# Dealing edges into buckets: running counts moved to TensorE, buffers and table pieces redistributed, loads of the joint stage reordered

## The chip, the core and the metric

The kernel runs on one core of a Trainium2 chip. Its engines are called here as the profile calls them: PE is TensorE's matmul (PEld its weight loads), DVE is VectorE, ACT is ScalarE, POOL is GpSimd, SP is SyncE, and a "q" behind a name marks a DMA issue on that engine's queue. The metric is the device time of one execution in microseconds (us), as a median of several. All times within a profile count from the start of the span of one profiled execution.

## The reference

A graph with N = 3125 nodes of 256 features and E = 53125 directed edges (with self loops) goes through four layers. The change touches the first of them and what feeds it:

```python
h        = relu(concat(node[src], node[dst], edge_attr) @ mW1 + mb1)   # per edge, 512 units
messages = h @ mW2 + mb2
agg      = segment_sum(messages, src, num_segments=N)
u        = relu(concat(node, agg) @ uW1 + ub1) @ uW2 + ub2
x        = x + node + u                                                # node = layernorm(x)
```

Three more layers follow: a mixture of four experts, two graph convolutions over the same edges (segment sums over the edge list, done as products with a dense matrix of edge counts), and a feed-forward layer for half of the tokens. None of these is changed.

## The kernel before

The first product is split: `concat(node[src], node[dst], edge_attr) @ mW1` is a table row of the source (`tab_a`), plus a table row of the target (`tab_b`), plus a small product of the edge's 16 attributes. Each table has one row of 512 values for each node. `tab_h` holds `tab_a` in two halves (a rounded value and the rest), and `w_h` holds the 16 rows of weights of the attributes in two halves as well.

**Dealing, `deal()`.** Edges are sorted by source into 98 buckets of 32 nodes. The edge list is laid out as 416 tiles of 128 edges, taken in 104 chunks of four. For each chunk:

- `buckets(c)` compares bucket numbers with a row of ids on DVE (`oh`, one-hot, 128 x 4 x 98, L340) and adds up, in four DVE adds (`so_far`, L346 and L350), how many edges of each bucket each partition had in all tiles before.
- `select(c)` makes two products on PE (L363, L364): a triangular matrix `later` with `oh`, and a matrix of ones with `so_far`. Their sum in PSUM is, for each edge and bucket, the number of edges before it.
- `place(c)` picks each edge's own bucket (`own`, L371; `ranks`, L374), computes its place in the buffer (L376 to L382, `to`) and builds the row to be stored: `rt`, of which DVE makes the one-hot source part (L385) and ACT copies attributes and target (L107). `to` and `rt` are rings of six buffers each.
- `put(c)` stores the four tiles with four indirect DMAs of POOL (L394) to `cbuf`, in HBM; each takes 128 rows to 128 computed places.

In the first 13 chunks `halve_attributes` also turns the edges' attributes on PE and splits them in two halves (L298 on ACT, L299 on DVE).

**Tables, `tables()`.** A generator in four pieces for each of 25 blocks of 128 nodes: layernorm rows on DVE (with one square root on ACT); turning them on PE and copying (ACT); the products with `mW1` on PE (L313), followed for `tab_a` by the addition of the bias on DVE (L316, the bias `mb1` loaded as 128 copies of its row), the rounded half on ACT (L318) and the rest on DVE (L319), and for `tab_b` by a copy on ACT; and five DMA writes on SP (L325 to L329). From chunk 4 on, two pieces are taken after each chunk, so a block takes two chunks and the tables end half way through the dealing.

The order of instructions on PE, DVE, ACT and SP is the order of the program text there: the loop calls `buckets(c+2)`, `select(c+1)`, `put(c)`, `place(c+1)`, then the table pieces. Behind the last chunk come the counts of all buckets and checks on DVE (`count` to `fits`, L422 to L447), and the writing of `w_h` (L450 to L454). `fits` decides at a branch which of two joint stages runs; here it is the fast one.

**Joint stage, `edges_by_bucket()`.** A unit g is a group of four buckets; it is worked on in five steps (ROUNDS). `begin(g)` loads with SP the unit's rows of `tab_h` (`gives`, two DMAs of 256 KB, L698) and its edges (`rows`, 680 KB, L700). `goes` (DVE, L706) makes indices from them, `fetch` gathers `tab_b` rows by four indirect DMAs of 256 KB a step on POOL (L713), three steps ahead, into four buffers. `turned` turns the one-hot and attribute part on PE (L735) and copies it on ACT (`oT`, L107), `spread` multiplies it by `gives` (PE, L752), `hidden_units` adds the gathered rows (DVE, L758), ACT applies the relu (L763) and `by_source` sums by source (PE, L769). From the second unit on, `counts` (the dense matrix of edge counts) and the nodes' own work run in between. `goes(1)` stands in the text behind the hidden units of step 2 and ahead of those of step 3; `begin(1)` stands in step 0.

Ahead of the steps, `rest_of(fast)` issues on ACT's queue 26 loads of weights and biases for the nodes' work (L468 to L497), then four zero fills of the count matrix (L680 to L686, also ACT); SP issues `begin(0)` and eight copies of `w_h` into `gives` (L842).

Of the kernel before, what the change touches and what calls it, by code (L numbers as in the profile page):

```python
# [8 lines left out]
F32 = mybir.dt.float32  # L9
# [7 lines left out]
P = 128  # L17
# [33 lines left out]
def gnn_ffn_kernel(ctx: ExitStack, tc: tile.TileContext, a: dict, out: bass.AP):  # L51
# [125 lines left out]
    def deal():  # L177
# [46 lines left out]
        for k in range(0, NB - 1, 8):  # L224
            nc.sync.dma_start(x[:, k:k + 8, :], a["x"][k * P:(k + 8) * P].rearrange("(k p) d -> p k d", p=P))
            if k == 0:
                mw1 = tp.tile([P, 4, HID], F32, name="mw1", bufs=1)
                nc.sync.dma_start(mw1, a["L0_gnn_mW1"][0:2 * D].rearrange("(k p) m -> p k m", p=P))
                mb1 = tp.tile([P, HID], F32, name="mb1", bufs=1)
                b = a["L0_gnn_mb1"]  # L230
                nc.sync.dma_start(mb1, bass.AP(tensor=b.tensor, offset=b.offset, ap=[[0, P], [1, HID]]))
                w_ea = tp.tile([32, HID], F32, name="w_ea", bufs=1)
                for i in range(2):
                    nc.sync.dma_start(w_ea[16 * i:16 * (i + 1)], a["L0_gnn_mW1"][2 * D:2 * D + 16])
# [67 lines left out]
        def tables():  # L302
            for k in range(NB):
                xns = layernorm_rows(k, 1, True, nc.vector)
                yield
                xT = tp.tile([P, 2, P], F32, name="xTa")
                layernorm_turn(xns, xT)
                yield
                ts = []
                for h in range(2):  # L310
                    pp = bank("pp")
                    for c in range(2):
                        nc.tensor.matmul(pp, lhsT=xT[:, c, :], rhs=mw1[:, 2 * h + c, :], start=c == 0, stop=c == 1)  # L313
# [12 lines left out]
                nc.sync.dma_start(tab_a[rows, :], ts[0])  # L326
                nc.sync.dma_start(tab_h[rows, 0, :], first.bitcast(F32))
                nc.sync.dma_start(tab_h[rows, 1, :], rest.bitcast(F32))
                nc.sync.dma_start(xT0[:, :, rows], xT)  # L329
                yield  # L330


        with tc.tile_pool(name="deal", bufs=3) as dp:
            chunks = ET // GB
            ohs, pos, rts = {}, {}, {}

            def buckets(c):

                oh = dp.tile([P, GB, NBK], F16, name="oh", bufs=4)
                nc.vector.tensor_tensor(oh, ids[:, :NBK].unsqueeze(1).to_broadcast([P, GB, NBK]),  # L340
                                        bk[:, c * GB:(c + 1) * GB].unsqueeze(2).to_broadcast([P, GB, NBK]), op=OP.is_equal)
                so_far = dp.tile([P, GB, NBK], F16, name="so_far", bufs=4)
                with nc.allow_low_precision("whole numbers up to 416"):
                    if c:
                        oh_, last = ohs[c - 1]
                        nc.vector.tensor_tensor(so_far[:, 0], last[:, GB - 1], oh_[:, GB - 1], op=OP.add)  # L346
                    else:
                        nc.vector.memset(so_far[:, 0], 0.0)
                    for i in range(1, GB):
                        nc.vector.tensor_tensor(so_far[:, i], so_far[:, i - 1], oh[:, i - 1], op=OP.add)  # L350
                ohs[c] = oh, so_far

            def edges_before(some):
                pk = bank("pk")
                nc.tensor.matmul(pk[:, :NBK], lhsT=ones, rhs=some, start=True, stop=True)
                return pk[:, :NBK]

            def select(c):

                oh, so_far = ohs[c]  # L360
                pk = bank("pk")
                out = pk[:, :GB * NBK].rearrange("p (g b) -> p g b", g=GB)
                nc.tensor.matmul(out, lhsT=later, rhs=oh, start=True, stop=False)  # L363
                nc.tensor.matmul(out, lhsT=ones, rhs=so_far, start=False, stop=True)  # L364
                return out

            def place(c, out):
                oh = ohs[c][0]
                at = slice(c * GB, (c + 1) * GB)
# [34 lines left out]
            for c in range(-1, chunks):  # L404
# [17 lines left out]
            oh, so_far = ohs[chunks - 1]  # L422
            run = dp.tile([P, NBK], F16, name="run", bufs=1)
            with nc.allow_low_precision("whole numbers up to 416"):
                nc.vector.tensor_tensor(run, so_far[:, GB - 1], oh[:, GB - 1], op=OP.add)
            count = dp.tile([P, NBK], F32, name="count", bufs=1)
            nc.vector.tensor_copy(count, edges_before(run))
            most = dp.tile([P, NBK], F32, name="most", bufs=1)
            nc.vector.tensor_scalar(most, count, float(CAP), None, op0=OP.is_gt, op1=OP.add, accum_out=bad[:, 0:1])
            nc.vector.tensor_scalar(most[:, :full * GB], count[:, :full * GB], float(SURE * P), None, op0=OP.is_lt, op1=OP.add,  # L430
                                    accum_out=bad[:, 1:2])

# [15 lines left out]


            wf, wr = [dp.tile([32, HID], F32R, name=f"w_{j}", bufs=1) for j in "hl"]  # L450
            nc.scalar.activation(wf, w_ea, AF.Copy)
            nc.vector.tensor_tensor(wr, w_ea, wf.bitcast(F32), op=OP.subtract)
            nc.sync.dma_start(w_h[:, 0, :], wf.bitcast(F32))
            nc.sync.dma_start(w_h[:, 1, :], wr.bitcast(F32))  # L454
        prep.close()
# [5 lines left out]
    def rest_of(fast):  # L461
# [211 lines left out]
        def edges_by_bucket():  # L673
            with tc.tile_pool(name="bk", bufs=2) as bp, tc.tile_pool(name="upd", bufs=2) as up, \
# [4 lines left out]

                for hf, w in ((half0, W0), (half1, W1)):  # L680
                    left = NP - NBK * BN
                    flat = hf[NBK * BN:, :].rearrange("s (h l) -> (s h) l", l=w)
                    cn = bp.tile([P, W1], F16, name="cn", bufs=5)
                    nc.vector.memset(cn, 0.0)
                    for o in range(0, 4 * left, P):
                        nc.scalar.dma_start(flat[o:o + P, :], cn[:, :w])  # L686

                gives = [bp.tile([P, 2, 2, HID], F32R, name=f"gives{i}", bufs=1) for i in range(2)]  # L690

                def begin(g):
                    nb = min(4, NBK - 4 * g)
                    ag = gives[g % 2]
                    for i in range(2):
                        src = bass.AP(tensor=tab_h.tensor, offset=tab_h.offset + (g * P + i * BN) * 2 * HID,
                                      ap=[[2 * HID, BN], [4 * BN * HID, nb // 2], [1, 2 * HID]])
                        nc.sync.dma_start(ag[2 * BN * i:2 * BN * i + BN, :nb // 2].bitcast(F32).rearrange("p i c h -> p i (c h)"), src)  # L698
                    rows = bp.tile([P, PER, RW], F32R, name="rows", bufs=3)
                    nc.sync.dma_start(rows.bitcast(F32).rearrange("p r w -> p (r w)"),  # L700
                                      cbuf[g * P * PER:(g + 1) * P * PER, :].rearrange("(p r) w -> p (r w)", p=P))
                    return dict(g=g, nb=nb, m=nb * BN, ag=ag, rows=rows, oa={}, ob={})
# [136 lines left out]
                for t in gives:  # L839
                    for at in (BN, 3 * BN):  # L840
                        for i in range(2):
                            nc.sync.dma_start(t[at:at + 32, i].bitcast(F32), w_h[:])  # L842


# [537 lines left out]
```

## Time and profile before

| | |
|---|---|
| runs | 2400.23, 2407.05 and 2401.82 us; median 2401.82 |
| the profiled execution | 2503.9 us, its span 2501.8 us |
| mean granted PE clock | 0.832 |
| busy in the span | PE 1836.7 us (73%), DVE 1549.4 (62%), POOL 987.6 (39%), ACT 876.3 (35%) |

The stages, with the share of time in which each engine was busy in them:

| stretch, us | what runs | PE | DVE | ACT | POOL | DMA | clock |
|---|---|---|---|---|---|---|---|
| 0 to 32 | loads, `cbuf` cleared, first chunks placed | 0.24 | 0.89 | 0.15 | 0.09 | 0.88 | 1.00 |
| 32 to 84 | dealing, attributes halved, first tables | 0.35 | 0.55 | 0.17 | 0.61 | 0.59 | 0.80 |
| 692 to 1790 | joint stage: edges, counts, nodes | 0.89 | 0.63 | 0.52 | 0.47 | 0.56 | 0.87 |
| 1790 to 1917 | last nodes, hand-over to the convolutions | 0.76 | 0.40 | 0.37 | 0.12 | 0.23 | 0.87 |
| 1917 to 2274 | two convolutions | 0.98 | 0.67 | 0.37 | 0.07 | 0.50 | 0.97 |
| 2274 to 2502 | ranking and the last layer | 0.80 | 0.54 | 0.18 | 0.00 | 0.04 | 0.90 |

The rest of the dealing and the hand-over (84 to 692) are taken up in the prediction. A row of the profile's table of groups reads: line, engine, operation, tile written and tiles read, count, then total busy time and the mean in nanoseconds of one, then the idle time of the engine just before such instructions and what ended it. Three groups of the dealing, over 0 to 660 us, are:

| group | count | busy us | mean ns |
|---|---|---|---|
| L350 DVE add, `so_far` | 312 | 66.4 | 213 |
| L346 DVE add, `so_far` of the next chunk | 103 | 21.1 | 205 |
| L313 PE, products of the tables | 200 | 133.1 | 826 |

A timeline row gives the start, the duration (of several merged instructions together, with their count behind an x), and in brackets how long the engine had been idle and what ended that. The name of a releaser is inferred from semaphore events; "issue" means that nothing in the profile ended the wait.

### The profile page before, as it was taken

How to read it: one execution, taken by the hardware profiler on the slowest of the kernel's cores; microseconds unless marked ns; L12 is line 12 of the kernel's file. 1: busy time of each engine (PE TensorE's matmuls, PEld its weight loads, DVE VectorE, ACT ScalarE, POOL GpSimd, SP SyncE). 2: the span in 40 equal slices, each digit the busy share in tenths (PEclk: the TensorE clock that was granted, in tenths of full speed). 3: DMA queues.
4: the chain of work that ended last, by engine and by line, in shares of the span. 5: the costliest groups of instructions: out<-in, count | busy, mean ns of one | idle time of the engine just before them, and what ended most of it. 6: DMA issues, size and time to landing. Idle time of an engine off the chain costs nothing. (4 is left out here: it accounts for less than half of the span.)

```text
span 2501.8 us, 26233 instructions
## 1 busy us (share of the span) xinstructions
PE 1836.7 (73%) x7873; PEld 1091.7 (44%) x7873; DVE 1549.4 (62%) x4427; ACT 876.3 (35%) x1553; POOL 987.6 (39%) x1032
## 2 busy tenths in 40 slices
PE   3455551111078898898898998898885999999689
PEld 1222220000034454455454454454454777886356
DVE  7687775555255665665665665665644676667931
ACT  1211110000045555555555555554433333343111
POOL 4566666766545444445444444444300000110000
PEclk9687775555568889889889899899897999999889
DMA  8233330000666556555555555555304444650000
GB/s 265 96 129 124 119 118 25 25 24 26 167 201 196 146 159 173 161 162 178 157 158 165 150 178 165 149 172 169 114 26 125 120 129 119 169 145 1 0 34 19
DMA packets 231403, 309.98 MB, mean 124 GB/s; under 512 B 34392, under 2 KB 165315, under 8 KB 230884
## 3 DMA queue, kind: packets, MB, share of 16 engines
q1 hardware_dynamic: 167296, 153.00, 20.8%
q0 software_dynamic: 52512, 142.96, 19.6%
q10 hardware_dynamic: 11444, 12.27, 1.6%
q8 instruction: 64, 1.05, 0.2%
q14 instruction: 87, 0.71, 0.1%
HBM read 226.44 MB, written 81.69 MB: 123 GB/s over the span
## 5 line engine op out<-in xcount | busy, mean ns | idle before, releaser
L713 POOL DMA_INDIRECT cb<-tab_b,goes_to x490 | 477.4, 974 | 617.8 <-issue 275.1
L394 POOL DMA_INDIRECT cbuf<-rt,to x416 | 416.3, 1001 | 233.3 <-issue 197.1
L758 DVE TENSOR_TENSOR cb<-pa,cb 128x1024 f32<-128x1024 f32 x245 | 288.7, 1218 | 263.2 <-PE pa L752 190.1
L1277 PE MATMUL padj<-z,slab 128*128 128x512 f32 x1250 | 321.4, 410 | 16.0 <-DVE z L1186 16.0
L763 ACT ACTIVATE cb<-cb 128x1024 f32<-128x1024 f32 x245 | 257.6, 1051 | 94.7 <-DVE cb L758 72.9
L1277 PEld LDWEIGHTS padj<-z,slab 128*128 128x128 f32 x1250 | 233.2, 192 | 75.4 <-issue 24.1
L752 PE MATMUL pa<-gives,oT 64*128 64x512 f32 x980 | 188.7, 506 | 36.1 <-ACT oT L107 34.3
L133 PE MATMUL pt<-ident,xn 128*128 128x128 f32 x200 | 49.5, 339 | 218.8 <-DVE xn L122 130.3
L363 PE MATMUL pk<-oh,later 128*128 128x392 f16 x104 | 47.2, 454 | 190.3 <-DVE oh L340 95.0
L810 PE MATMUL pn<-ob,oa 128*128 128x448 f16 (+1 forms) x692 | 165.6, 363 | 20.6 <-ACT cn L107 7.5
L125 POOL TENSOR_TENSOR x<-x,xn 128x256 f32<-128x256 f32 x25 | 24.4, 978 | 352.7 <-DVE xn L122 352.7
L795 DVE TENSOR_SCALAR ob<-ids,rows 128x448 f16<-128x448 f16 (+1 forms) x490 | 163.3, 333 | 0.0
L791 DVE TENSOR_SCALAR oa<-ids,rows 128x128 f16<-128x128 f16 x692 | 163.0, 262 | 0.0
L752 PEld LDWEIGHTS pa<-gives,oT 64*128 64x128 f32 x980 | 105.8, 231 | 101.2 <-ACT oT L107 43.8
L769 PE MATMUL ph<-cb,rows 128*32 128x512 f32 x980 | 144.8, 645 | 0.0
L107 ACT ACTIVATE oT<-pt 64x256 fp32r<-64x256 f32 (+1 forms) x250 | 93.1, 373 | 134.9 <-DMA cb<-tab_b,goes_to 72.2
L107 ACT ACTIVATE cn<-pn 128x352 f16<-128x352 f32 x196 | 98.3, 502 | 118.0 <-PE pn L810 91.0
L313 PE MATMUL pp<-mw,xTa 128*128 128x512 f32 x200 | 133.1, 826 | 0.2 <-issue 0.2
L133 PEld LDWEIGHTS pt<-ident,xn 128*128 128x128 f32 x200 | 24.8, 160 | 243.1 <-DVE xn L122 129.5
L107 ACT ACTIVATE rt<-row 128x144 f32<-128x144 f32 x104 | 32.8, 319 | 258.7 <-DMA cbuf<-rt,to 208.1
L506 PE MATMUL pd<-xT,fw 128*128 128x512 f32 (+1 forms) x224 | 91.8, 566 | 35.4 <-DVE y L1328 35.4
L735 PEld LDWEIGHTS pt<-ident_r,rows 128*128 128x128 f32 x490 | 67.1, 198 | 110.4 <-issue 69.4
(221 smaller groups left out, 3137.4 us busy)
## 6 DMA issues: line engine op xcount, KB each, us to landing
two<-adj_h SPq DMA_DIRECT2D x24, 1600.0 KB
rows<-cbuf SPq DMA_DIRECT2D x25, 680.0 KB
gives<-tab_h SPq DMA_DIRECT2D x48, 256.0 KB
adj_h<-cn SPq DMA_DIRECT2D x98, 112.0 KB
adj_h<-cn SPq DMA_DIRECT2D x98, 88.0 KB
cb<-tab_b,goes_to POOLq DMA_INDIRECT x490
cbuf<-rt,to POOLq DMA_INDIRECT x416
cbuf<-empty ACTq DMA_DIRECT2D x4, 1632.0 KB
```

The lines of the kernel that those rows point to most:

```text
L107: nc.scalar.activation(dst, src, AF.Copy)
L313: nc.tensor.matmul(pp, lhsT=xT[:, c, :], rhs=mw1[:, 2 * h + c, :], start=c == 0, stop=c == 1)
L394: one_of = nc.gpsimd.indirect_dma_start(out=cbuf[:], out_offset=bass.IndirectOffsetOnAxis(ap=to[:n, i:i + 1], axis=0), in_=rt[:n, i, :], i ...
L713: nc.gpsimd.indirect_dma_start(out=cb[:, j, :], out_offset=None, in_=tab_b[:], in_offset=bass.IndirectOffsetOnAxis(ap=u["to"][:, i:i + 1], ...
L752: nc.tensor.matmul(got[j // 2][:, j % 2, :], lhsT=oT[at, j // 2, :], rhs=u["ag"][at, j // 2, c, :], start=c == 0, stop=c == 1)
L758: nc.vector.tensor_tensor(cb[:, j:j + 2], pa, cb[:, j:j + 2], op=OP.add)
L763: nc.scalar.activation(h, h, AF.Relu)
L769: nc.tensor.matmul(u["ph"][j * BN:(j + 1) * BN, :], lhsT=u["rows"][:, GB * r + j, :BN].bitcast(F32), rhs=hs[j // 2][:, j % 2, :], start=r ...
L791: nc.vector.tensor_scalar(oa, ids[:, 1 + i * P:1 + (i + 1) * P], field[:, 0:1], None, op0=OP.is_equal)
L795: nc.vector.tensor_scalar(ob[:, :w], ids[:, 1:w + 1], field[:, 1:2], None, op0=OP.is_equal)
L810: nc.tensor.matmul(pn[:, :w], lhsT=u["oa"].pop((j, r, i)), rhs=u["ob"][j, r][:, :w], start=r == rs[0], stop=r == rs[-1])
L1277: nc.tensor.matmul(pa, lhsT=slab[:, c, :], rhs=(z2 if second else z1)[:, c, :], start=c == 0, stop=c == NB - 1)
```

## The change

It has five parts, all of them up to and including the start of the joint stage.

1. The four DVE adds of `so_far` go. `select(c)` sums the earlier tiles of its own chunk with three products of ones by shifted parts of `oh`, and all earlier chunks with a product of one row of ones by a row of totals. The totals (1 x 98) are carried from chunk to chunk: four products of a column of ones by the chunk's tiles, one product that adds the totals before, and a copy on ACT.
2. The bias of `tab_a` is loaded as one row and added on PE as a product of a row of ones by it; ACT copies the result out of PSUM.
3. `to` and `rt` get rings of 20 buffers; tables are made one piece a chunk from chunk 3 on.
4. `w_h` is written at the third chunk instead of behind the last one; the last counts come out of the totals, on one partition.
5. In the joint stage the 26 loads are held back and issued on SP behind `begin(0)` and the copies of `w_h`; the zero fills follow them, on SP as well; `begin` loads `rows` ahead of `gives`.

```diff
-                mb1 = tp.tile([P, HID], F32, name="mb1", bufs=1)
-                b = a["L0_gnn_mb1"]
-                nc.sync.dma_start(mb1, bass.AP(tensor=b.tensor, offset=b.offset, ap=[[0, P], [1, HID]]))
+                mb1 = tp.tile([1, HID], F32, name="mb1", bufs=1)
+                nc.sync.dma_start(mb1, a["L0_gnn_mb1"].rearrange("(o m) -> o m", o=1))
+                one_row = tp.tile([1, P], F32, name="one_row", bufs=1)
+                nc.vector.memset(one_row, 1.0)
...
-                        nc.tensor.matmul(pp, lhsT=xT[:, c, :], rhs=mw1[:, 2 * h + c, :], start=c == 0, stop=c == 1)
+                        nc.tensor.matmul(pp, lhsT=xT[:, c, :], rhs=mw1[:, 2 * h + c, :], start=c == 0, stop=h == 1 and c == 1)
+                    if h == 0:
+                        nc.tensor.matmul(pp, lhsT=one_row, rhs=mb1, start=False, stop=True)
                     t = tp.tile([P, HID], F32, name=f"t{h}")
+                    copy(t, pp)
                     if h == 0:
-                        nc.vector.tensor_tensor(t, pp, mb1, op=OP.add)
                         first, rest = [tp.tile([P, HID], F32R, name=f"t0{j}") for j in "hl"]
-                        nc.scalar.activation(first, t, AF.Copy)
+                        copy(first, t)
                         nc.vector.tensor_tensor(rest, t, first.bitcast(F32), op=OP.subtract)
-                    else:
-                        copy(t, pp)
...
-                so_far = dp.tile([P, GB, NBK], F16, name="so_far", bufs=4)
-                with nc.allow_low_precision("whole numbers up to 416"):
-                    if c:
-                        oh_, last = ohs[c - 1]
-                        nc.vector.tensor_tensor(so_far[:, 0], last[:, GB - 1], oh_[:, GB - 1], op=OP.add)
-                    else:
-                        nc.vector.memset(so_far[:, 0], 0.0)
-                    for i in range(1, GB):
-                        nc.vector.tensor_tensor(so_far[:, i], so_far[:, i - 1], oh[:, i - 1], op=OP.add)
-                ohs[c] = oh, so_far
+                ohs[c] = oh
...
-                oh, so_far = ohs[c]
+                oh, so_far = ohs[c], totals.pop(c - 1, None)
...
-                nc.tensor.matmul(out, lhsT=ones, rhs=so_far, start=False, stop=True)
+                for k in range(1, GB):
+                    nc.tensor.matmul(out[:, k:], lhsT=ones, rhs=oh[:, :GB - k], start=False, stop=c == 0 and k == GB - 1)
+                if c:
+                    nc.tensor.matmul(out, lhsT=ones[:1], rhs=so_far.unsqueeze(1).to_broadcast([1, GB, NBK]), start=False, stop=True)
+                pt = bank("ptot")
+                for i in range(GB):
+                    nc.tensor.matmul(pt[:1, :NBK], lhsT=ones[:, :1], rhs=oh[:, i], start=i == 0, stop=c == 0 and i == GB - 1)
+                if c:
+                    nc.tensor.matmul(pt[:1, :NBK], lhsT=ones[:1, :1], rhs=so_far, start=False, stop=True)
+                if c + 1 < chunks:
+
+                    totals[c] = dp.tile([1, NBK], F16, name="total")
+                    copy(totals[c], pt[:1, :NBK])
...
-                to, f = dp.tile([P, GB], I32, name="to", bufs=6), dp.tile([P, GB], F32, name="f")
+                to, f = dp.tile([P, GB], I32, name="to", bufs=20), dp.tile([P, GB], F32, name="f")
...
-                rt = dp.tile([P, GB, RW], F32, name="rt", bufs=6)
+                rt = dp.tile([P, GB, RW], F32, name="rt", bufs=20)
...
-                if c >= 4:
-                    for _ in range(2):
-                        next(making, None)
+                if c == 2:
+
+                    wf, wr = [dp.tile([32, HID], F32R, name=f"w_{j}", bufs=1) for j in "hl"]
+                    nc.scalar.activation(wf, w_ea, AF.Copy)
+                    nc.vector.tensor_tensor(wr, w_ea, wf.bitcast(F32), op=OP.subtract)
+                    nc.sync.dma_start(w_h[:, 0, :], wf.bitcast(F32))
+                    nc.sync.dma_start(w_h[:, 1, :], wr.bitcast(F32))
+                if c >= 3:
+                    next(making, None)
...
-        queue[0] = nc.scalar if fast else nc.sync
+        held = []
+
+        class Held:
+            @staticmethod
+            def dma_start(to, src):
+                held.append((to, src))
+
+        if fast:
+            queue[0] = Held
...
                 def begin(g):
                     nb = min(4, NBK - 4 * g)
                     ag = gives[g % 2]
+                    rows = bp.tile([P, PER, RW], F32R, name="rows", bufs=3)
+                    nc.sync.dma_start(rows.bitcast(F32).rearrange("p r w -> p (r w)"),
+                                      cbuf[g * P * PER:(g + 1) * P * PER, :].rearrange("(p r) w -> p (r w)", p=P))
...
-                    rows = bp.tile([P, PER, RW], F32R, name="rows", bufs=3)
-                    nc.sync.dma_start(rows.bitcast(F32).rearrange("p r w -> p (r w)"),
-                                      cbuf[g * P * PER:(g + 1) * P * PER, :].rearrange("(p r) w -> p (r w)", p=P))
...
                             nc.sync.dma_start(t[at:at + 32, i].bitcast(F32), w_h[:])
+                for to, src in held:
+                    nc.sync.dma_start(to, src)
+
+                for hf, w in ((half0, W0), (half1, W1)):
...
+                        nc.sync.dma_start(flat[o:o + P, :], cn[:, :w])
```

More of the change, by code (lines that the diff above doesn't have):

```diff
@@ L334, in deal @@
             chunks = ET // GB
-            ohs, pos, rts = {}, {}, {}
+            ohs, totals, pos, rts = {}, {}, {}, {}
             def buckets(c):
@@ L341, in buckets @@
                                         bk[:, c * GB:(c + 1) * GB].unsqueeze(2).to_broadcast([P, GB, NBK]), op=OP.is_equal)
-                so_far = dp.tile([P, GB, NBK], F16, name="so_far", bufs=4)
-                with nc.allow_low_precision("whole numbers up to 416"):
-                    if c:
-                        oh_, last = ohs[c - 1]
-                        nc.vector.tensor_tensor(so_far[:, 0], last[:, GB - 1], oh_[:, GB - 1], op=OP.add)
-                    else:
-                        nc.vector.memset(so_far[:, 0], 0.0)
-                    for i in range(1, GB):
-                        nc.vector.tensor_tensor(so_far[:, i], so_far[:, i - 1], oh[:, i - 1], op=OP.add)
-                ohs[c] = oh, so_far
[L353 to L356, printed above, removed]
+                ohs[c] = oh
             def select(c):
-                oh, so_far = ohs[c]
+                oh, so_far = ohs[c], totals.pop(c - 1, None)
                 pk = bank("pk")
@@ L363, in select @@
                 nc.tensor.matmul(out, lhsT=later, rhs=oh, start=True, stop=False)
-                nc.tensor.matmul(out, lhsT=ones, rhs=so_far, start=False, stop=True)
+                for k in range(1, GB):
[10 more added lines that the diff above has]
+                    copy(totals[c], pt[:1, :NBK])
+                else:
+                    totals[c] = dp.tile([1, NBK], F32, name="count", bufs=1)
+                    copy(totals[c], pt[:1, :NBK])
                 return out
             def place(c, out):
-                oh = ohs[c][0]
+                oh = ohs[c]
                 at = slice(c * GB, (c + 1) * GB)
@@ L414, in deal @@
                     place(c + 1, sel)
-                if c >= 4:
-                    for _ in range(2):
-                        next(making, None)
+                if c == 2:
[6 more added lines that the diff above has]
+                    next(making, None)
                 if c + 2 < chunks:
                     ohs.pop(c, None)
[L422 to L429, printed above, removed]
+            for _ in making:
+                pass
+            count = totals[chunks - 1]
+            most = dp.tile([1, NBK], F32, name="most", bufs=1)
+            nc.vector.tensor_scalar(most, count, float(CAP), None, op0=OP.is_gt, op1=OP.add, accum_out=bad[:1, 0:1])
             nc.vector.tensor_scalar(most[:, :full * GB], count[:, :full * GB], float(SURE * P), None, op0=OP.is_lt, op1=OP.add,
-                                    accum_out=bad[:, 1:2])
+                                    accum_out=bad[:1, 1:2])
             nc.vector.tensor_scalar(low, d_f, float(H0), None, op0=OP.is_lt)
@@ L447, in deal @@
             nc.vector.tensor_scalar(fits, pf[:1, :1], 0.5, None, op0=OP.is_lt)
[L450 to L454, printed above, removed]
         prep.close()
@@ L678, in edges_by_bucket @@
                 st["up"] = up
[L680 to L686, printed above, removed]
                 gives = [bp.tile([P, 2, 2, HID], F32R, name=f"gives{i}", bufs=1) for i in range(2)]
@@ L842, in edges_by_bucket @@
                             nc.sync.dma_start(t[at:at + 32, i].bitcast(F32), w_h[:])
+                for to, src in held:
+                    nc.sync.dma_start(to, src)
+                for hf, w in ((half0, W0), (half1, W1)):
+                    left = NP - NBK * BN
+                    flat = hf[NBK * BN:, :].rearrange("s (h l) -> (s h) l", l=w)
+                    cn = bp.tile([P, W1], F16, name="cn", bufs=5)
+                    nc.vector.memset(cn, 0.0)
+                    for o in range(0, 4 * left, P):
+                        nc.sync.dma_start(flat[o:o + P, :], cn[:, :w])
                 es.enter_context(tc.manual_schedule())
```

## The prediction

> **What bounds the kernel now.** I read the page first (slices, groups), then the timelines of POOL and DVE while edges are dealt, the busy times by stretch, and the timeline around the hand-over to the joint stage.
>
> ```profile
> L394 POOL DMA_INDIRECT cbuf<-rt,to x416 | 416.3, 1001 | 233.3 <-issue 197.1
> ```
>
> 416 indirect puts (104 chunks of four) make up the dealing. The first starts at 32.61, when the clearing writes to `cbuf` have landed; the last ends at 653.0. By stretches (us; busy and count for PE, PEld, DVE, ACT, POOL; PE clock, DMA share, GB/s):
>
> ```profile
> 84.00:358.00 274.00, 153.36 (x328) 65.36 (x325) 216.19 (x742) 55.32 (x139) 184.52 (x180) 0.78 0.36 121
> 358.00:653.00 295.00, 53.77 (x113) 12.99 (x113) 173.72 (x672) 17.88 (x55) 200.04 (x205) 0.51 0.11 35
> 653.00:692.00 39.00, 1.09 (x4) 0.93 (x4) 0.66 (x3) 0.34 (x1) 15.22 (x16) 0.50 0.96 245
> ```
>
> The stretch with tables (to 358) needs 274/180 = 1.52 us a put, and there POOL waits once a chunk or two for DVE: two chunks and one table take DVE from 206.18 to 218.53, 12.35 us. Afterwards POOL runs back to back (0.96 busy, 0.30 between) for 28 puts and stops for 5 us:
>
> ```profile
> 424.15 0.96 POOL L394 DMA_INDIRECT cbuf<-rt,to  x1 [0.30 <-issue]
> 429.52 0.96 POOL L394 DMA_INDIRECT cbuf<-rt,to  x1 [4.41 <-issue]
> ...
> 460.51 0.21 DVE L350 TENSOR_TENSOR so_far<-so_far,oh 128x98 f16<-128x98 f16 x1 [1.19 <-DVE so_far L350]
> 461.91 0.21 DVE L350 TENSOR_TENSOR so_far<-so_far,oh 128x98 f16<-128x98 f16 x1 [1.19 <-DVE so_far L350]
> ```
>
> In these spells DVE waits 0.5 to 3.9 us for its own previous result, at starts that are multiples of 0.70 us apart. That is a late semaphore, not a full ring of six buffers: at 446.8 DVE is only two chunks ahead. Seven such stops and one of 8.2 us at 68 cost POOL some 38 us. I see this lateness only while POOL issues indirect DMAs (none after about 1850), and the profiled execution (2503.9; span 2501.8) is 102 us over the median 2401.8, so I count most of it to the profiled execution. Without it the last put would end near 603: puts of the last chunk with a table end at 365, less the 12.8 us DVE stood still at 60 to 72.9, plus 196 puts at 1.28 (251 us).
>
> The hand-over:
>
> ```profile
> 658.04 0.35 SPq L700 DMA_DIRECT2D rows<-cbuf  x1
> 664.63 0.18 DVE L706 CAST goes_to<-rows 128x20 int32<-128x20 f32 x1 [6.88 <-DMA rows<-cbuf]
> 684.27 7.29 ACTq L686 DMA_DIRECT2D adj_h<-cn  x4
> 691.66 0.78 ACT L107 ACTIVATE oT<-pt 64x256 fp32r<-64x256 f32 x2 [72.22 <-DMA cb<-tab_b,goes_to]
> ...
> 694.52 0.34 SPq L700 DMA_DIRECT2D rows<-cbuf  x1
> ```
>
> ACT issues 26 weight loads and 4 zero fills from 646.2 to 691.56, and only then turns `oT`, though its product on PE was done at 665.8 and the first gathers started at 665.79. The name of the DMA in the brackets misleads: ACT's own queue was the wait. The hidden units (DVE L758) of steps 0, 3 and 5 start at 694.18, 711.99 and 726.69. Below, T is the end of the last put (653.0 here), so these are T+41, T+59, T+74.
>
> **The change, part by part.**
>
> *Running counts on PE.* Out go four DVE adds a chunk: from the start of the first at 214.30 to `own` at 215.21, 0.91 us. A chunk without a table takes DVE 3.66 (220.57 to 224.23), so 2.75 is left. In come 3 `ones` products (588 columns), 1 broadcast (392) and 5 of 98 columns on PE. The cold row is 0.33 us for 392 columns (50.57 to 50.89), so 1470 columns are 1.24; with `later` 1.6, with weight loads some 2.3. PE had 0.7 a chunk.
>
> *Tables one piece a chunk*: four chunks a table instead of two, so POOL's period for them is 4 x 5.15 = 20.6. DVE over four chunks: 4 x 2.75 = 11.0; norm 1.98 (211.84 to 213.82); `t0l` 0.69; plus waits. The bias add (0.69) becomes a product with one row: the table's 8 matmul passes took 4.66 to 5.73, so 2 more are 1.2 to 1.4 us of PE, and ACT gets one more copy (0.60). `t0l` then waits for six passes (3.8), copy 0.6 and `first` 0.63, 5.2 in all, of which 2.75 is covered by placing: 2.4 uncovered. Behind it, `own` of the next chunk waits for four more passes and the select, about 1.5. Sum 17.7 against 20.6: DVE has 14% in hand and POOL becomes the bound. Here the rule on the clock is weighed: the Trainium skill (TensorE: Matmul & The Clock Gate, What's actually happening) says the default clock is half and activity releases it, which speaks against spreading PE's work thin. The rows: granted 0.78 with tables every 12 us, 0.51 without. By the first the PE figures shrink by a quarter and the sum is nearer 16.5; by the rule it stays 17.7, which I took. Either hides under POOL; if the cover went (above 5.97 a chunk, 620/104), all gain here would be gone.
>
> *Twenty buffers* let DVE run ahead, as ACT did with six; they issue nothing. Worth nothing where POOL is the bound without pauses, at most the 38 us of stops if the lateness also occurs in timed runs.
>
> *w_h at the third chunk* moves a wait: `w_ea` lands at 51.7 (last increment of its semaphore). ACT (`wf`) and DVE (`wr`) stand until about 51; queued behind them are chunk 4's attributes, `rt` and totals. Four chunks are placed by then, which feed POOL to 32.6 + 20.6 = 53.2; chunk 4 is ready near 55.6, and until chunk 12 DVE halves attributes too (0.69 each), level with POOL. I take 5 us lost (0 to 10). SP's two `w_h` writes move past table writes and cost nothing there; 256 KB of broadcast bias less are 1 us at most.
>
> *Dealing in sum*: a put costs 1.28 (200.04/205 + 0.30) to 1.33 (184.52/180 + 0.30); I take 1.295, nearer the first, as DVE loses half its two-input work: 32.6 + 5 + 416 x 1.295 = 576. Against 603: **-27**; at the ends -33 and -12. Last count and checks stay in DVE's lead over POOL (13 us now, at least one chunk after).
>
> *Hand-over.* SP now issues rows, gives, 8 `w_h`, 26 weights, 4 fills, then the second unit's rows. Puts no longer share with weights: rows issue at T+2 (now T+5), land by T+6, first gathers at T+7, step 0 at about T+15 instead of T+41, step 2 at T+27. But `goes(1)` (DVE L706) precedes step 3 in DVE's order and needs the second rows, now last in SP's queue. Ahead of them: 680 + 512 + 1024 + 4370 + 400 + 680 KB = 7.85 MB, plus 20 gathers of 256 KB (5.24 MB) on POOL's queue. At the 245 GB/s of the third stretch above that is 53 us: T+55. Step 3 then at T+55.5 (now T+59), step 5 at T+67 (T+74) with 5.9 us a step: 7; with the rows at T+51, 11. I take **-8**. Here rule and row differ: the skill (DMA: Bandwidth & Descriptors, Issuing engines are not separate DMA queues) says that all queues share the same 16 engines, and that another issuer saves only sequencer time. ACT's thirty issues sum to 15.3 us, so by the rule -15; by the row of `oT` -26. The rule's other half, shared engines, is why I take less than both: what frees ACT stands in front of SP's rows. Ends: +8 (rows at T+70) and -26.
>
> **Sum**: -27 - 8 = -35, 2401.8 - 35 = **2367**. In a profiled execution the last put may move from 653 to anything between 576 (lateness gone) and 637 (28 puts every 40.3 us, as now); its span is no check on the forecast.
>
> **Rivals.**
> 1. *SP's queue eats the hand-over*: second rows at T+70 or later. For: SP waits for earlier loads between its issues (6.2 us once), and the eight `w_h` issues took 18.7 us. Against: 245 GB/s. -27 + 8: 2383.
> 2. *DVE or PE remains the bound*: the table chain's waits are doubled (four waits of 2 more us each four chunks, 20 to 24): puts at 1.45, dealing about level, -8: 2394.
> 3. *Slower*: the late semaphores are in timed runs too, and now strike while tables run. A late spell lasts some 21 us in each 40 and lets DVE do 2 chunks; the 19 us left give 4.3 at 17.7/4, so 6.3 a chunk, and 104 x 6.3 + 38 = 693 against 653: +40 - 8, 2434. It decides from 5.97 us a chunk. For: POOL at full rate is what precedes each spell. Against: fewer DVE results to signal, and the missing 102 us.
> 4. *More*: lateness in timed runs, but the lead of up to twenty chunks carries POOL over it: up to 653 - 576 = 77, with 8 to 26: 2299 to 2317.
>
> **Chances**: forecast (2350 to 2380) 0.51; rival 1 0.17, 2 0.11, 3 0.10, 4 0.11. Range 2310 to 2396: it leaves out 3 and half of 4. Faster by over 0.3% (7.2 us, what a measurement can tell from none) takes the forecast, 1, 4 and half of 2: 0.85; same 0.05; slower 0.10.
>
> **What would show it.** Right: L350 gone, POOL's idle before L394 at 0.30 almost everywhere from 80 on, tables through the whole dealing, `oT` within 15 us of T, and a wait of DVE L706 for the second rows of 20 us or more. Wrong: POOL waiting 1 us or more each chunk on DVE (rival 2), the second rows landing at T+70 (1), or before T+40, which would make the hand-over worth over 20.

## The result, and the profile after

| | runs | median, us | ratio to before, 95% interval |
|---|---|---|---|
| before, measured beside it | 2400.23 to 2407.05 | 2404.14 | |
| after | 2376.01, 2377.61, 2380.51, 2382.64 | 2379.06 | 0.9897 [0.9875, 0.992] |
| after, a second time | 2369.11 to 2378.79 | 2377.89 | 0.9875 [0.9853, 0.9897] |

The ratios and intervals are those on record; they can differ from the ratio of the two medians by up to 0.002. The change gains 25 us, where 35 were forecast; its median lies 1 us inside the forecast's band (2350 to 2380), which is less than its own interval. The profiled execution of after has a span of 2373.7 us and none of the late semaphores that the profile of before was full of.

The dealing's group on the page of after (columns as before), and the busy times by stretch (PE, PEld, DVE, ACT, POOL; clock, DMA share, GB/s):

```profile
L396 POOL DMA_INDIRECT cbuf<-rt,to x416 | 413.2, 993 | 165.9 <-issue 97.5
```

```profile
84.00:200.00 116.00, 90.68 (x334) 38.55 (x333) 80.29 (x265) 28.14 (x85) 87.51 (x90) 0.69 0.27 88
350.00:500.00 150.00, 118.63 (x448) 49.63 (x448) 110.13 (x370) 37.35 (x112) 115.24 (x115) 0.70 0.29 96
500.00:582.60 82.60, 0.19 (x2) 0.11 (x2) 3.09 (x9) 0.00 (x0) 62.74 (x66) 0.50 0.10 32
582.60:622.00 39.40, 20.46 (x76) 10.71 (x76) 9.17 (x10) 9.36 (x14) 18.97 (x20) 0.54 1.00 309
```

POOL now stores from 33.1 to 582.6 without a stop but for four, all before 120: 3.2 us at 53.6, 5.6 at 72.5, 0.9 and 1.0 later. The third row shows what sets the end: DVE, PE and ACT have finished the last chunk by 500, and POOL works through what the twenty buffers hold. DVE's row for the early `w_h`, and the hand-over (T is 582.6) on DVE and SP:

```profile
52.08 0.68 DVE L421 TENSOR_TENSOR w_l<-w_ea,w_h 32x512 fp32r<-32x512 f32 x1 [19.10 <-ACT w_h L420]
...
597.85 1.23 DVE L757 TENSOR_TENSOR cb<-pa,cb 128x1024 f32<-128x1024 f32 x1 [9.50 <-DMA cb<-tab_b,goes_to]
...
618.62 0.49 SPq L695 DMA_DIRECT2D rows<-cbuf  x1
...
626.27 0.18 DVE L705 CAST goes_to<-rows 128x20 int32<-128x20 f32 x1 [10.74 <-DMA rows<-cbuf]
```

Step 0 comes at T+15.3. The indices of the second unit wait 10.7 us for rows that SP could issue only at T+36, behind the 26 loads and the zero fills; they come at T+43.7.

### The profile page after: what moved, and what is told of

Read it like the earlier page. It is cut to its first block, busy times and chain, and to the rows that moved or that the text cites. A ratio compares the mean times of both kernels' runs of the same rounds, so it can differ in the third digit from the quotient of the medians.

```text
span 2373.7 us, 27598 instructions
## 1 busy us (share of the span) xinstructions
PE 1949.7 (82%) x8752; PEld 1149.2 (48%) x8752; DVE 1451.3 (61%) x3985; ACT 908.2 (38%) x1682; POOL 985.2 (42%) x1032
## 5 line engine op out<-in xcount | busy, mean ns | idle before, releaser
L751 PE MATMUL pa<-gives,oT 64*128 64x512 f32 x980 | 183.4, 493 | 23.3 <-ACT oT L107 21.6
L734 PE MATMUL pt<-ident_r,rows 128*128 128x128 f32 x490 | 83.2, 293 | 85.0 <-DMA gives<-tab_h 85.0
L314 PE MATMUL pp<-mw,xTa 128*128 128x512 f32 x200 | 148.1, 882 | 0.0
L1214 ACT ACTIVATE slab<-two 128x2048 fp32r<-128x2048 f16 x50 | 95.6, 1911 | 40.6 <-PE padj L1287 38.8
L117 ACT ACTIVATE rstd<-mv,eps 128x1 f32<-128x1 f32 (+1 forms) x76 | 22.4, 295 | 231.3 <-DVE mv L115 231.2
```

The lines of the kernel that those rows point to most:

```text
L734: nc.tensor.matmul(pt[:, j * P:(j + 1) * P], lhsT=flat[:, at:at + P], rhs=ident_r, start=True, stop=True)
L751: nc.tensor.matmul(got[j // 2][:, j % 2, :], lhsT=oT[at, j // 2, :], rhs=u["ag"][at, j // 2, c, :], start=c == 0, stop=c == 1)
```

## The experiments

The kernel before was timed beside each group of experiments, on the same chip; the groups ran on four chips. It took 2405.64 us beside the first four kernels and 2403.89 beside the next four, but 2486.40 and 2489.95 beside the last ones. I come to these two chips at the end.

**The kernel before, profiled again.** No edit.

> The kernel before, profiled once more. Theory (the late semaphores belong to that one profiled execution, not to the kernel): no waits of DVE in steps of 0.70 us, a span near 2402 instead of 2501.8, and the last put at about 603 us. Rival (the kernel brings the lateness about whenever its puts run back to back): stops of 4 to 5 us every 28 puts again, last put at about 650. If the first holds, this profile is the one to compare with the kernel after.

It took 2401.61 us, span 2399.5, with no late semaphore. A stretch and DVE at the hand-over:

```profile
358.00:604.80 246.80, 45.10 (x95) 9.51 (x94) 163.36 (x628) 14.39 (x44) 187.65 (x195) 0.50 0.12 37
```

```profile
636.42 2.35 DVE L758 TENSOR_TENSOR cb<-pa,cb 128x1024 f32<-128x1024 f32 x2 [21.78 <-PE pa L752]
...
654.23 2.36 DVE L758 TENSOR_TENSOR cb<-pa,cb 128x1024 f32<-128x1024 f32 x2 [3.47 <-PE pa L752]
```

The last put ends at 604.8 (603 was worked out), and behind the tables POOL runs without a stop: 246.8 us for 195 puts are 1.27 us each. POOL's 24 gaps (35.0 us in all) all lie before 356, where two table pieces follow each chunk. Step 0 is at T+31.6 and step 3 at T+49.4, both 10 us less than in the profile the prediction had.

**The two halves alone.** First all but part 5; then part 5 alone:

```diff
 # after, part 5 undone
-        if fast:
-            queue[0] = Held
+        queue[0] = nc.scalar if fast else nc.sync
...
 # before, with part 5
-        queue[0] = nc.scalar if fast else nc.sync
+        if fast:
+            queue[0] = Held
...
```

> The changed dealing alone; the loads of the joint stage stay on ACT's queue and in the old order. Theory: the dealing is worth 20 us (603 to 582.6 for the last put), so 2384 against 2404, and the last put ends at 583 +/- 3. Rival (POOL was nearly the bound before, the gain is the hand-over's): within 5 us of before. Since weights are read while the last puts land, oT comes some 35 us or more behind the last put, as before.

> The old dealing with the new order of loads at the start of the joint stage. Theory: 5 to 8 us less than before (2396 to 2399), because DVE waits at L706 for the second unit's rows behind 26 loads. Rival: the first oT comes 20 us or more earlier behind the last put and all of it counts, 2380 to 2384.

The dealing alone: 2378.74 us, ratio 0.9895 [0.9878, 0.9912], 26.9 us gained, last put at 576.8. The hand-over alone: 2399.22 us, 0.9979 [0.997, 0.9988], 6.4 us gained; step 0 at T+15.8, but step 3 at T+44.7, only 4.7 us earlier than in the kernel before. The last put of the first, and what DVE waits for ahead of step 3 in the second (T is 605.5):

```profile
575.98 0.86 POOL L396 DMA_INDIRECT cbuf<-rt,to  x1 [0.30 <-issue]
...
650.10 0.18 DVE L707 CAST goes_to<-rows 128x20 int32<-128x20 f32 x1 [11.08 <-DMA rows<-cbuf]
```

By the medians each half comes within 2 us of its term, and their sum is 33.3 against the 25 of the whole. Whether they really fail to add is taken up below.

**The second unit's rows ahead of the held loads**, on top of after:

```diff
+                units[1] = begin(1)
                 for to, src in held:
                     nc.sync.dma_start(to, src)
...
-                    if r == 0 and g + 1 < NB:
+                    if r == 0 and 0 < g and g + 1 < NB:
```

> The kernel after, with the second unit's rows and gives issued ahead of the 26 held loads. Theory: the wait of DVE L705 for rows (10.7 us in the profile after) goes, step 3 comes 9 to 11 us earlier, 2368 to 2371 against 2379. Rival (the DMA engines are the limit, and bytes taken out of one wait come back in the gathers): under 4 us gained, and the hidden units of steps 3 to 5 wait for gathers instead.

2362.03 us, 0.9821 [0.9805, 0.9837]: 17 us better than after by the medians. In the profiles the hand-over shows 7 of them (step 10 at T+73.1 instead of T+80.3). The last put also comes 3 us earlier (579.2), but nothing was edited there: the stop at 72.5 us was 1.3 us long in this execution instead of 5.6. DVE at its second unit:

```profile
612.46 0.17 DVE L705 CAST goes_to<-rows 128x20 int32<-128x20 f32 x1
614.54 2.36 DVE L757 TENSOR_TENSOR cb<-pa,cb 128x1024 f32<-128x1024 f32 x2 [1.92 <-PE pa L751]
```

No bracket behind L705: the rows are there before they are asked for, and step 3 starts at T+35.3 instead of T+43.8. So SP's order had taken back most of what freeing ACT gave: 12 us at step 10 with the rows first (T+85.1 in the kernel before), 2 to 5 without.

**The spreading of the tables alone**, on the kernel before:

```diff
-                if c >= 4:
-                    for _ in range(2):
-                        next(making, None)
+                if c >= 3:
+                    next(making, None)
...
+            for _ in making:
+                pass
```

> The kernel before, with the tables one piece a chunk (from the fourth chunk on) instead of two and nothing else: the running counts stay on VectorE, six buffers stay, the four loads and the zero fill stay. Theory A, the spreading carries the gain of the dealing: per four chunks VectorE has 4 x 3.66 + 1.98 + 3.0 = 19.6 us of work against 20.4 us of GpSimd's sixteen puts, so it keeps up by a hair; the 24 gaps of GpSimd (35.0 us in the kernel before) all but vanish, the last put ends at 575 to 582 instead of 604.8, and the time falls by 22 to 29 us (2376 to 2383). Rival B, VectorE must lose the counts as well: margins of 4% don't last through the lumps of a table's pieces, GpSimd still stops every few chunks, now over twice the stretch, the last put ends at 590 or later and the time falls by less than 15 us (above 2390).

2363.05 us, 0.9829 [0.981, 0.9847]: this alone gains 41 us, more than the whole change. On the page, and among ACT's waits from 100 to 600 (us in total, times, longest):

```profile
L394 POOL DMA_INDIRECT cbuf<-rt,to x416 | 410.4, 987 | 156.3 <-issue 96.7
```

```profile
ACT rt L107 <- DMA cbuf<-rt,to: 242.5, 62, 5.2
```

POOL never stops from 33.2 to 570.2. ACT stands 242.5 us because all six buffers are full: the makers wait for POOL, with the counts still on DVE. The time fell by 12 us more than theory A had. The spans of the two profiles differ by 39.9: 34.6 up to the last put (604.8 to 570.2), 1.6 from there to step 10, and 3.6 behind it, where the two kernels have the same instructions. That last part I could not place.

**Six buffers instead of twenty**, on after, and **after once more**, unedited, beside it:

```diff
-                to, f = dp.tile([P, GB], I32, name="to", bufs=20), dp.tile([P, GB], F32, name="f")
+                to, f = dp.tile([P, GB], I32, name="to", bufs=6), dp.tile([P, GB], F32, name="f")
...
-                rt = dp.tile([P, GB, RW], F32, name="rt", bufs=20)
+                rt = dp.tile([P, GB, RW], F32, name="rt", bufs=6)
```

> The changed kernel with six buffers for rows and places instead of twenty. Theory A, GpSimd sets the pace and never waits, so the lead VectorE builds up is worth nothing: within 3 us of the changed kernel (2376 to 2382), last put at 577 to 583; VectorE is done with its last chunk near 560 instead of 500. Rival B, the lead is what rides over the lumps of the table pieces: GpSimd stops once in each table, some 1 us times 17 tables, last put near 600, and the time is 15 us or more above the changed kernel's.

> The changed kernel once more, beside the versions above. Its parts measured alone sum to 27 + 6 = 33 us, it alone gained 25. Theory A, the products of the first table ran on a slow TensorE clock in its profile by chance (last put at 582.6 where the same dealing ended at 576.8 and 579.2 in two other profiles): this profile's stop at 72 us is 1 to 3 us and the last put ends at 576 to 580; the time stays at 2376 to 2382 as the executions mix. Rival B, the 5.6 us are there in each execution of this kernel: last put at 582 again.

Six buffers: 2371.20 us, 0.9856 [0.9832, 0.9879]; twenty: 2377.89, 0.9875 [0.9853, 0.9897]. Neither theory had six better. The intervals overlap, so the time alone doesn't show it; the puts do. Both profiles have the same stops (3.25, 2.1 and 0.8 us, 6.2 in all), yet the last put ends at 572.0 against 578.3. The groups, six and then twenty:

```profile
L396 POOL DMA_INDIRECT cbuf<-rt,to x416 | 406.9, 978 | 161.7 <-issue 102.8
```

```profile
L396 POOL DMA_INDIRECT cbuf<-rt,to x416 | 413.0, 993 | 161.9 <-issue 98.9
```

15 ns a put, 416 times, are the 6 us. The mean is 992 to 997 ns in all five profiles with twenty buffers and without late semaphores, and 978 here. Puts that overlap one of DVE's one-hots (L341, 0.56 us each) last 1.087 us in the mean in the kernel with twenty (105 puts) and 1.016 with six (125); the others last 0.961 and 0.962. So with twenty fewer puts meet a one-hot, but at worse moments: 60 of them last over 1.0 us, with six 37.

As to the stop at 72 us, after's second profile had 2.1 us of it instead of 5.6, as theory A said. The products of the first table took 3.62, 2.07 and 3.78 us in the first profile, 3.62, 1.50 and 1.98 in the second, and 2.95, 1.12 and 1.98 in the dealing alone. The third of them, in the first and then in the second profile:

```profile
67.00 3.78 PE L314 MATMUL pp<-mw,xTa 128*128 128x512 f32 x4
...
66.39 1.98 PE L314 MATMUL pp<-mw,xTa 128*128 128x512 f32 x4
```

The same instructions take twice as long, as at half a clock. The column of the granted clock doesn't show it: it reads 1.00 from 60 to 72 in all three profiles, so the clock as the cause is read from the lengths alone.

**`w_h` after chunk 41 instead of after chunk 3**, on top of the rows-first version:

```diff
-                if c == 2:
+                if c == 40:
```

> The version with the second unit's rows ahead of the held loads, and the two halves of the edge weights written after chunk 41 instead of after chunk 3. Theory: VectorE and ScalarE no longer stand still from 33 to 52 us for that weight's load, so GpSimd's two stops at 53 and 72 us (4.5 us together in that version's profile, 8.8 in the changed kernel's) go; the last put ends near 574 and the time is 3 to 6 us below 2362 (2356 to 2359). Rival: VectorE then stands still as long for the other weights of the first table, which come in the same row of loads, and the stops stay: 2362.

2359.51 us, 0.9815 [0.9797, 0.9833]. All of POOL's stops are gone (4.6 us before) and the last put ends at 572.2 instead of 579.2. The two spans differ by 6.2 us, the medians by 2.5, with overlapping intervals, so no gain in time is shown. DVE's row shows that the rival was half right, as it now waits for the nodes' rows of the first table:

```profile
48.79 0.43 DVE L114 BATCH_NORM_STATS2 st<-x 128x6 f32<-128x256 f32 x1 [11.88 <-DMA x<-in_x_dram]
```

But by then it has placed one chunk more, and that covers POOL.

**Combinations, and what another chip makes of them.** Three more kernels: the dealing alone with the late `w_h`; the last version with six buffers; and the kernel before with only spread tables, rows-first hand-over and late `w_h`. The third ran once more on another chip. The first two repeat edits shown above; the third, against before, is in its main lines (the rest of part 5 is as in the change):

```diff
+                if c == 40:
+                    wf, wr = [dp.tile([32, HID], F32R, name=f"w_{j}", bufs=1) for j in "hl"]
...
+                if c >= 3:
+                    next(making, None)
...
+                units[1] = begin(1)
+                for to, src in held:
+                    nc.sync.dma_start(to, src)
...
```

> The dealing of the change alone (counts on TensorE, twenty buffers, spread tables; hand-over as before), with the halves of the edge weights written after chunk 41. Theory A, what the changed dealing loses against the kernel with spread tables alone (2363, last put 570.2) is that weight's early wait: GpSimd's stops at 53 and 72 us go, the last put ends at 570 to 573 and the time comes to 2363 to 2370, from 2378.7 for the same dealing with the early write. Rival B, counts on TensorE and twenty buffers cost something behind the dealing as well: last put at 570 to 573, but the time stays at 2372 to 2376.

> The best version so far (2359.5: the change, second unit's rows first, edge weights after chunk 41) with six buffers instead of twenty. Theory A, a put lasts longer while VectorE makes its one-hots beside it, and with six buffers fewer of them meet: mean put 978 ns instead of 992, so the last put ends 5 to 7 us earlier (565 to 568) and the time is 2352 to 2356. Rival B, six buffers gained 6.7 us in the earlier pair by chance of the executions: last put at 571 to 573, time 2358 to 2362.

> The kernel before with only its tables spread (one piece a chunk), the change's reordered loads with the second unit's rows first, and the edge weights written after chunk 41: counts on VectorE, six buffers. Theory A, counts on TensorE carry nothing: last put at 569 to 572, step 10 at 71 to 74 us behind it, time 2349 to 2358, no worse than the version with the counts on TensorE (2359.5). Rival B, the two parts don't add because VectorE is late at the end of the dealing: first step 25 us or more behind the last put, time 2360 or more.

> The kernel before with its tables spread, the change's reordered loads with the second unit's rows first, and the edge weights after chunk 41 (counts on VectorE, six buffers), once more. On the last chip the kernel before took 2486 and stops of all engines' semaphores cost it, and this version 0.5%. Theory A, those stops belong to a chip: where the kernel before takes about 2404 they are absent, the last put ends at 569 to 572, step 10 lies 71 to 74 us behind it, and the time is 2349 to 2358 (2% below before). Rival B, this version makes the stops itself: the last put ends after 600 and the gain is below 1% wherever it runs.

| | counts on | us | ratio to before there, 95% interval | last put |
|---|---|---|---|---|
| dealing alone, late `w_h` | PE | 2529.38 | 1.0171 [1.0148, 1.0194] | 690.8 |
| rows first, late `w_h`, six buffers | PE | 2514.06 | 1.0108 [1.0083, 1.0133] | 693.8 |
| spread tables, rows first, late `w_h` | DVE | 2474.63 | 0.9951 [0.9932, 0.997] | 652.1 |
| the same again | DVE | 2464.19 | 0.9906 [0.9878, 0.9934] | 637.4 |

All four fell on chips where the kernel before takes 2486 and 2490 us, so none answers its question; what they show is another. The late semaphores are back in all four profiles, and the kernel before is slow there in every one of its 17 and 11 timed runs (2473 to 2496), near the 2503.9 of its first, disturbed profile. Those runs left no trace, so that the same lateness slowed them is inferred. From the first of them, the waits from 100 to 600, and PE and then DVE at one stop:

```profile
DVE own L373 <- remote: 141.5, 18, 8.8
...
PE pk L354 <- ACT total L107: 132.4, 19, 8.8
ACT total L107 <- remote: 111.0, 19, 8.7
```

```profile
242.59 0.33 PE L354 MATMUL pk<-total,ones 1*128 1x392 f16 x1
...
250.31 0.57 DVE L373 TENSOR_TENSOR own<-pk,oh 128x392 f32<-128x392 f32 x1 [7.49 <-remote]
```

PE has finished the counts at 242.92; DVE, which needs nothing else, learns of it at 250.31. A table takes four chunks and meets one such stop, 18 or 19 of them in 500 us, and DVE's period for four chunks is 25.3 us instead of the 17.1 of after. POOL gets through sixteen puts in some 20.5 (16 times 0.98 and 0.30), so it waits for DVE again. The pages of the second and third kernel:

```profile
L396 POOL DMA_INDIRECT cbuf<-rt,to x416 | 406.7, 978 | 283.7 <-issue 166.9
```

```profile
L394 POOL DMA_INDIRECT cbuf<-rt,to x416 | 406.7, 978 | 242.0 <-issue 191.2
```

A put costs the same; POOL's idle time is 42 us more where the counts are on PE. There DVE's period is 25.3 us, with the counts on DVE 23.8. These two kernels ran on one chip and differ in parts 1 and 2 and in the last counts alone: the work moved from DVE costs 39 us there (2514.06 against 2474.63). In the first kernel PE's next counts wait for the total that ACT copies (132.4 us above); one late signal there holds up the counts of the next chunk. That this is why they suffer more is argued, not tried. Nor did after itself run on such a chip, or the last version on one of the first kind; theory A of its second run was neither borne out nor refuted.

## Why the prediction was right, and where it was not

- **The bound and the dealing.** Right in size and in mechanism: 603 to 576 was forecast, 604.8 to 576.8 measured with the dealing alone (582.6 and 578.3 in the two profiles of after). The put's 1.295 us is (582.6 - 33.1 - 10.7)/416 = 1.295. DVE takes 17.1 us for four chunks, between the 17.7 taken and the 16.5 of a faster clock; with the tables spread the granted clock is 0.69 and 0.70 instead of 0.78, so spreading did thin it out. POOL becomes the bound. The early `w_h` costs 4.5 us (3.25 + 1.24, dealing alone) to 8.8 (3.25 + 5.6); 5 was said. Of the five signs named, four came (L350 gone, POOL's idle at 0.30, tables through the whole dealing, `oT` at T+7.3); the wait for the second rows was 10.7 us, not 20.
- **Which part carries it.** The prediction charged the dealing to all parts together. The spreading alone does it, and the prediction's own figures had it: 12.35 us of DVE for two chunks and a table, and 2 x 3.66 for two more chunks, are 19.7, below POOL's 20.6. Counts on PE give DVE a lead that nothing needs on the first two chips, twenty buffers make a put 15 ns longer (worth nothing, I had said; the last put comes 6.3 us later), and the early `w_h` stops POOL twice.
- **The hand-over, -8.** Alone it gained 6.4 by the medians, 2.9 to 7.2 by the interval, by a step whose two ends were both wrong. "T+41, T+59, T+74" for steps 0, 3 and 5 came from a disturbed execution: I took the late semaphores out of the dealing but left them in the hand-over. In the clean profile they are T+31.6, T+49.4 and T+58.3. And the second rows came at T+44, not T+55, since the stretch moved 309 GB/s, not 245. That the two errors cancel is luck. The mechanism, that they wait behind SP's 26 loads, held, and the rows-first run shows its price. What the freed queue of ACT gave ahead of that is nearer the row's 26 than the 15 of the summed issues: `oT` moved from T+29.1 to T+7.3.
- **The sum, -35.** It is 10 us more than the 25 measured, and it simply adds -27 and -8. By the medians the halves gain 26.9 and 6.4 and the whole 25.1 and 26.0, so nothing of the hand-over seems left. By the intervals that isn't shown: 1.05% and 0.21% are 1.26% together, and the whole has 1.03% [0.8, 1.25] and the second time 1.25% [1.03, 1.47]. In the profiles step 10 starts at 689.9 in the kernel before, at 662.2 with the dealing alone, 686.6 with the hand-over alone, 662.8 and 661.1 in after. The halves' 27.7 and 3.3 are 31.0, the whole has 27.1 and 28.8, and the later last put of after's two profiles (5.7 and 1.5 us), most of it the stop at 72 us, covers most of the difference. Behind step 10 single profiles settle nothing: the kernel before, the dealing alone and the spreading alone have the same instructions there and take 1710, 1716 and 1706 us. How much of the 10 us is halves that don't add, and how much scatter, stays open.
- **Slips in its working.** The stops behind 358 are six, not seven (29.5 us; with the 8.2 at 68 they are the 38). Rival 2's sum leaves out the start: 32.6 + 416 x 1.45 is 636, 33 us behind 603 and not level with it, so that rival stood at about 2427, beyond the range.
- **The late semaphores.** "Most of it to the profiled execution" held for the comparison asked for, and was too narrow. They are in all four profiles on two other chips; whether the chips make them or what else ran there at the time, the runs don't tell apart. There the third rival's figures come out nearly to the digit: 6.3 us a chunk and a last put at 693 were written down, 6.3 (25.3/4) and 690.8 and 693.8 measured; +40 without the hand-over, +43 measured with the dealing alone and the late `w_h`. That is luck in part: it had spells of 21 us in each 40, and the trace has one stop of some 8 us in each table (141.5 us in 18). The prediction gave it one chance in ten, because the timed runs lacked those 102 us. That was evidence about the runs shown, and I read it as evidence about the kernel.

## What to carry to other kernels

Before adding work to relieve an engine, see whether it is late because of its load or because the load is bunched in one half of the stage: one piece a chunk instead of two gained more alone than together with counts on another engine and more buffers. When loads are moved off a blocked queue, put what the next step needs ahead of them. When a profile is disturbed, clean every stage of it or none, and time a change on more than one chip: where signals between engines come late, work handed from engine to engine can cost more than it saves.

## What the runs showed of the hardware

A put is slowed when DVE, beside it, runs an instruction with two inputs in SBUF. In the second profile of after, puts that overlap a one-hot last 1.087 us in the mean against 0.961. Sharper is the comparison of puts shortly before which (0.05 to 0.35 us) DVE starts an instruction: with the one-hot (two inputs in SBUF, 0.56 us) all 44 last over 1.0 us, 1.19 in the mean, and with `t0l` (two, 0.69 us) all 5, 1.31; with `own` (0.56 us, one of its inputs in PSUM) 13 last 0.957, and with `ranks` (0.56 us, one input) 24 last 0.958. `rt` (two inputs, but 0.28 us) hardly shows: 0.978. The Trainium skill (SBUF — State Buffer, SBUF: two separate sides) says that DVE and GpSimd share a pair of ports which one holds for a whole instruction while the other stands, among others where DVE has two inputs in SBUF, as the one-hot has. That agrees: the longest put beside a one-hot in any profile took 1.51 us, 0.55 more than 0.96, just below one such instruction.

On two of the four chips of these experiments DVE and ACT waited up to 8.8 us at a time for results that were done (the rows above), and PE for ACT behind them, nearly all of it while POOL stored. The kernel before is 3.5% slower there (2486 and 2490 against 2404 and 2406). Versions with spread tables gain 1.0 to 1.9% elsewhere, and those that ran on these two lie between 1.7% slower and 0.9% faster; no version but the kernel before ran on both kinds.
